# A window-attention and Fourier-mixing kernel: its output turned by VectorE and stored in 16 transfers a band, its planner's count changed

## The chip, the cores and the metric

The kernel runs on one core of a Trainium2 chip. The metric is the device time of one execution in microseconds. All data are float32, apart from a small bias product in bfloat16.

## The reference

The input x is [8, 192, 64, 64]: 8 images, 192 channels, 64 x 64 tokens. Two layers follow one another.

```python
# layer 0
s = layer_norm(tokens)                      # over the 192 channels
q, k, v = qkv(windows of 8 x 8 tokens of s) # 6 heads of 32
a = normalize(q) @ normalize(k).T * temperature
a = where(a >= its 16th largest in the row, a, -100)
x2 = s + proj(softmax(a + rpb) @ v)
x2 = x2 + fc2(gelu(fc1(layer_norm(x2))))    # hidden 768
# layer 1
f = fft2(layer_norm(x2))                    # over 64 x 64, per channel
f = two-layer net on (real, imag) of each value, hidden 16, gelu
y = x2 + ifft2(f).real
out = y + mlp2(gelu(mlp1(layer_norm(y))))   # hidden 768, biases included
```

The output has channels first again, [8, 192, 64, 64].

## The kernel before

Each image is cut into 8 bands of 8 image rows, 512 tokens; so there are 64 bands. A band goes through `front` (load, turn to tokens, layer norm, q, k and v), two `attention` halves, and `back` (projection, the first MLP, statistics for layer 1). When all bands of an image are through, 12 blocks of 16 channels go through `forward`, `pointwise` and `inverse`: the Fourier transform and its inverse as matrix products, with the small net between. Then `leave` takes each band j of image b through the second MLP and out.

Both MLPs are in `mlp` (L743). It takes token-major data (128 tokens on the partitions, 384 numbers of two token groups side by side), normalizes into xa, and turns it to channel-major hn. For layer 1, and for layer 0 from image 1 on, the turn goes over DRAM: VectorE transposes 32 x 32 blocks (lt, L756), SP writes them with four transfers (lr, L765) and fetches them with three (hn, L768 and L770). The first product is mh (L807 and L820), its gelu is on ScalarE (L791), and the second product is mo (L853), token-major again in PSUM.

In `leave` VectorE then adds mo and the residual xy into zt (L1479). TensorE transposes zt with six instructions into the PSUM tile pz (`to_channels`, L731 and L736), ScalarE adds the last bias MLP2B while it moves pz into z (L1491), and SP stores z with three transfers (L1494 and L1496), contiguous over 256 or 512 tokens of a channel.

Tags name pools of buffers: ps, four PSUM tiles that all products share; hn, two channel-major strips (used by hn and by z); att, five tiles (attention scores, their transposes, and lt); h, seven tiles of gelu results; xa, two.

The order is made by a planner in the kernel's own Python code, before anything is recorded. Every step is a `yield op(engine, weight, ...)` with an engine, a duration in units of 10 ns, the buffers it takes and frees, and what it waits for. `Plan.run` (L215) steps through these, engine by engine, choosing by a key that is the possible start plus the task's place, where a place is the image number with fractions for the band or block. `Plan.search` (L278) looks 4000 units ahead 80 times with random noise on the keys, values each draw by TensorE's weight inside that horizon plus 0.15 times that of the others, runs 2000 units with the best, and goes on. The result is an order for every engine, SP's queue included; the queues run in that order, and each instruction waits for its data. Buffers that a step frees come back 15 units after its end, 150 after a DMA.

The constants of layer 1 are loaded in `setup_layer1` (L606), all inside one step that the planner counts as 0 on GpSimd. The gains n1g go there in eight transfers of single numbers (L640). The weights of the second MLP, wmlp, are loaded at its end by `load_mlp` (L458), also uncounted.

Of the kernel before, what the change touches and what calls it, by code (L numbers as in the profile page):

```python
# [9 lines left out]
FP = mybir.dt.float32  # L10
# [3 lines left out]
ALU = mybir.AluOpType  # L14
# [115 lines left out]
class Plan:  # L130
# [84 lines left out]
    def run(self, until, noise=None):  # L215
        ops, clock, mode, units = self.ops, self.clock, self.mode, self.units
        at, front, place, ready = self.at, self.front, self.place, self.ready
        while ready:
# [48 lines left out]
            for name in put:  # L267
                units[name].append(end + (150 if engine == "sp" else 15))
                units[name].sort()
# [7 lines left out]

    def search(self, tries=80, step=2000, horizon=4000, spread=25):  # L278
        draw = random.Random(1)
        now = 0  # L280
        while self.ready:
            now = max(now, self.clock["pe"])
            kept, best = self.save(), None
            for k in range(tries):
                seed = draw.random()
                noise = drawn(seed, spread) if k else None
                if not self.run(now + horizon, noise):
                    self.restore(kept)
                    continue
                worth = 0  # L290
                for _, _, engine, begin, weight in self.log[kept[-1]:]:
                    part = min(weight, max(0, now + horizon - begin))
                    worth += part if engine == "pe" else 0.15 * part
                if not self.ready:
                    worth = 1e9 - max(self.clock.values())
                if best is None or worth > best[0]:
                    best = worth, seed if k else None
                self.restore(kept)
            seed = best[1]
            self.run(now + step, drawn(seed, spread) if seed is not None else None)  # L300
            now += step
        return [(self.names[task], engine, number) for number, task, engine, _, _ in self.log]


# [37 lines left out]
def program(ctx, tc, x, out, w):  # L342
# [108 lines left out]
    for h in range(6):  # L451
        src = bass.AP(w["rpb"].tensor, w["rpb"].offset + h * 225, [[15, 8], [1, 8], [1, 113]])
        nc.sync.dma_start(rrev[64 * (h // 3) : 64 * (h // 3) + 64, h % 3, 0:113], src)
    wides = spare("wides", [128, 3, 2, 128])
    qb_parts = spare("qb_parts", [1, 3, 2 * C], BF)
# [12 lines left out]
    for t in range(2):  # L468
# [5 lines left out]
    wproj = [ctile(f"wprojr_{k}", [128, 64 + C]) for k in range(2)]  # L474
    alongs = {name: ctile(name, [128, 2 * C]) for name in ("gain1", "bias1", "bias2")}
    gain1, bias1, bias2 = (
        t.unsqueeze(1).to_broadcast([128, 2, 2 * C]) for t in alongs.values()
# [40 lines left out]
    def setup_rows():  # L518

        yield op("pe", 20, "full", get="ps", after=["vbias", (None, 1700)])
        pv = psum("pvp")
        times(pv[:, 0, 0:1], wproj_raw, slice(0, CA), vbias)
        times(pv[0:64, 1, 0:1], wproj_raw, slice(CA, C), vbias)
        yield op("dve", 90, put="ps")
        for k, n in enumerate((CA, 64)):
            for v in (pv[0:n, k, 0:1], vec(B1)[k][0:n]):
                nc.vector.tensor_tensor(pbias[k][0:n], pbias[k][0:n], v, ALU.add)


        yield op("dve", 110, put="h h")
        for k, t in enumerate(wproj):
            nc.vector.tensor_copy(t[:, 64:], wproj_raw[k])
            nc.vector.tensor_copy(t[:, 0:64], wproj_raw[k][:, CA:C])
        vectors = (vec(G1), pbias, vec(FC2B))
        yield op("dve", 150)
        for wide, v in zip((wides[:, i] for i in range(3)), vectors):
            for k, n in enumerate((CA, 64)):
                nc.vector.tensor_copy(wide[0:n, k, :], v[k][0:n].to_broadcast([n, 128]))  # L540
        yield op("pe", 60, "full", get="ps", put="h")
        pt = psum("along")
        for i in range(3):
            for k, n in enumerate((CA, 64)):
                to = pt[:, i // 2, i % 2 * C + k * CA : i % 2 * C + k * CA + n]
                nc.tensor.transpose(to, wides[0:n, i, k, :], ident[0:n, 0:n])
        yield op("dve", 270, put="ps", done="rows")
        for i, t in enumerate(alongs.values()):
            of = pt[:, i // 2, i % 2 * C : (i % 2 + 1) * C]
            nc.vector.tensor_copy(t[:, 0:C], of)  # L550
            nc.vector.tensor_copy(t[:, C : C + 64], of[:, CA:C])
            nc.vector.tensor_copy(t[:, C + 64 :], of[:, 0:CA])
# [53 lines left out]
    def setup_layer1():  # L606
        yield op("pool", 0, get="xf", after=[("att", 0, 0, 1)])
        for j, name in enumerate(("fcos", "fsin")):
# [3 lines left out]
            for e in range(2):  # L612
                own = w[name][64 * e : 64 * e + 64]
                for c in range(2):
                    rows = 64 * c + 32 * e
                    nc.sync.dma_start(ihalf[j][rows : rows + 32], own[0:32])

        for t in range(4):
            row = 64 * (t % 2) + 32
            nc.sync.dma_start(ihalf[1][32 * t : 32 * t + 1], w["fcos"][row : row + 1])  # L620
        for k in range(4):
            src = w["fwd2"].rearrange("(a b k e) v -> k b a e v", a=2, k=4, e=2)[k]
            nc.sync.dma_start(frow[8 * k : 8 * k + 8], src)
        for c in range(1, 4):
            nc.sync.dma_start(frow[32 * c : 32 * c + 32], frow[0:32])
        inv1 = sb.tile([128, 128], FP, tag="xf", name="inv1", bufs=1)
        nc.sync.dma_start(inv1, w["inv1"])
# [4 lines left out]
        nc.sync.dma_start(ab, w["ab"])  # L632
        n1t = w["n1"]
        for c in range(2):
            for k in range(4):
                src = bass.AP(
                    n1t.tensor, n1t.offset + c * 2 * HC + k, [[0, 32], [4, 24], [1, 1]]
                )
                dst = n1g[32 * k : 32 * k + 32, 24 * c : 24 * c + 24]
                nc.sync.dma_start(dst.unsqueeze(2), src)  # L640
            nc.sync.dma_start(n1b2[:, c, :], w["n1"][c : c + 1, 1, :])
        yield op("dve", 120, after=[("att", 0, 1, 1)])
        for e in range(2):
# [29 lines left out]
        nc.vector.tensor_scalar(dc, ab[0:1, 1:2], float(HW), None, ALU.mult)  # L673
        nc.vector.tensor_scalar(n1b2, n1b2, float(HW), None, ALU.mult)
        wmlp.extend(load_mlp("wmlp1", "wmlp2"))

# [63 lines left out]
    def flat(name):  # L740
        return psum(name).rearrange("p k n -> p (k n)")

    def mlp(src, nm, w1, fc1_bias, w2, by_dma, then=None):  # L743

# [6 lines left out]
        if by_dma:  # L751
            ready = yield op("dve", 101, get="att rows", put="xa", after=last)
            turned = sb.tile([128, 6, 2, 2, 32], FP, tag="att", name=f"lt_{nm}", bufs=ATT_BUFS)
            whole = to.rearrange("p j (g k) -> p j g k", k=32)
            for t, g, c, n in ((0, 0, 0, 6), (1, 6, 4, 2), (1, 8, 0, 4)):
                nc.vector.transpose(  # L756
                    turned[:, c : c + n, t].rearrange("p g j k -> p j g k"),
                    whole[:, :, g : g + n],
                )
            yield op("sp", 200, put="att")  # L760
# [100 lines left out]
        return acc, last  # L861


    def loading(b, i):
# [5 lines left out]
    def front(b, i):  # L870
# [97 lines left out]

        def by_block(half, p):

            return half.rearrange("c (n b) -> c b n", b=2)[:, p]

        def qk_a(pq, p, first):
            for t in range(2):
                tok = by_block(xn[:, t * HALF : (t + 1) * HALF], p)
                nc.tensor.matmul(  # L976
                    pq[:, t, : 2 * C],
                    tok,
                    wqkv[0][:, : 2 * C],
                    start=first,  # L980
                    stop=not first,
                    skip_group_check=True,
                )

        def qk_b(pq, p, first):
            flags = dict(skip_group_check=True, stop=not first)
            for t in range(2):
                rows = slice(64 * t, 64 * t + 64)
                tok = by_block(xn[rows, BAND:ROW], p)
# [100 lines left out]
    def attention(b, i, hb):  # L1090
# [41 lines left out]
        for k0 in range(0, 12, 2):  # L1132
            yield op("dve", 90, get="sm" if k0 == 0 else "")
            if k0 == 0:
                top = small([128, 3, 4, 16], "top")
            rows = [(s[:, k // 4, k % 4], top[:, k // 4, k % 4]) for k in (k0, k0 + 1)]
            rest = [
                sb.tile([128, 64], FP, tag="s2", name=f"s2_{nm}_{k0 + k}", bufs=4) for k in range(2)
            ]
# [322 lines left out]
    def leave(b, j):  # L1462
# [3 lines left out]
        if j == 0:  # L1466
# [4 lines left out]
        yield op("pool", 0, after=blocks + [("dc", b), ("mlp", 1)])  # L1471
        xy = xys[b][0]
        acc, last = yield from mlp(
            lambda t, q: xy[:, t, q, j, :], f"d{nm}", wmlp[0], fcb[:, 1, :], wmlp[1], True
        )
        left[b] -= 1
        yield op("dve", 88, get="xa", put="ps xy" if left[b] == 0 else "ps")
        zt, pair = tokens("xa", 2, f"zt_{nm}")
# [4 lines left out]
            ALU.add,  # L1483
        )
        yield op("pe", 66, "full", get="ps hn", put="xa")
        pz = flat(f"pz_{nm}")
# [27 lines left out]
        ([(setup_layer1(), 0.2)], 1),  # L1514
        ([(setup_mlp(1, lambda: wmlp, *layer1, ["layer1", ("att", 0, 5, 1)]), 0.2)], 1),
        ([(front(b, i), at_band(b, i, -.12)) for b, i in bands], 1),
# [88 lines left out]
```

## Time and profile before

| | us |
|---|---|
| median of 3 runs | 4598.14 |
| lowest and highest | 4592.67, 4598.62 |
| profiled execution | 4606.84 |
| its span | 4605.0 |
| TensorE busy | 4377.8 |
| VectorE busy | 2769.9 |
| ScalarE busy | 2506.5 |
| GpSimd busy | 2337.6 |
| mean granted TensorE clock | 0.984 |

The profile is one execution; its span runs from the first to the last instruction. PE is TensorE, PEld its weight loads, DVE VectorE, ACT ScalarE, POOL GpSimd, and SPq the queue from which SP issues DMAs. A line of a group names the source line, engine, operation, written and read tile and shape; then busy time, mean duration in ns, and the idle time just before it with what ended it. A float32 product counts two instructions in the profile, a transpose one. In a table by stretches each engine has its busy time and its number of instructions; behind them stand the granted clock, the mean busy share of the 16 DMA engines and GB/s. In a timeline a line has the start, the length, the engine, and how many instructions were merged. For a tile's or a line's instructions the durations are lowest, median and highest in ns.

### The profile page before, as it was taken

Reading aid. Unit: us, or ns where it says so; the run is one execution under the profiler, and the core shown is the slowest. Engines: PE = TensorE matmul, PEld = TensorE weight load, DVE = VectorE, ACT = ScalarE, POOL = GpSimd, SP = SyncE. Lnnn points to the kernel's source line nnn. Section 1 sums busy time; section 2 is a strip of 40 time slices with the busy share of each in tenths; the row PEclk is TensorE's granted clock in tenths of the full one; section 3 lists DMA queues with packets and bytes.
Section 4 is the critical chain, followed back from the end, with each engine's and each line's share of the span. In section 5 each row is a group of like instructions: output and inputs, shape, how many; then the busy total and the mean of one; then the engine's idle time right before and its main releaser. Section 6 shows DMA issues by size and latency. Waiting matters only on the chain. (4 is left out here: it accounts for less than half of the span.)

```text
span 4605.0 us, 143865 instructions
## 1 busy us (share of the span) xinstructions
PE 4377.8 (95%) x60506; PEld 3470.0 (75%) x60506; DVE 2769.9 (60%) x11070; ACT 2506.5 (54%) x3693; POOL 2337.6 (51%) x2161
## 2 busy tenths in 40 slices
PE   7888999999999999999999999999999999999989
PEld 5777777887778777778767877778777787778758
DVE  7888776746774466763767456774576744742111
ACT  4555666545663456544656446564566544653552
POOL 7787765525564365652756246663375533631100
PEclk8999999999999999999999999999999999999999
DMA  2001221311123111221122211222112221111002
GB/s 55 16 12 50 57 60 41 98 52 43 50 57 94 49 47 47 67 73 50 47 56 63 71 50 54 57 64 71 56 47 57 74 63 43 47 47 52 19 19 66
DMA packets 271072, 246.42 MB, mean 54 GB/s; under 512 B 39983, under 2 KB 223482, under 8 KB 270426
## 3 DMA queue, kind: packets, MB, share of 16 engines
q1 hardware_dynamic: 270414, 237.22, 18.6%
q8 instruction: 476, 7.80, 0.7%
q14 instruction: 170, 1.39, 0.1%
q10 hardware_dynamic: 12, 0.00, 0.0%
HBM read 120.52 MB, written 116.39 MB: 51 GB/s over the span
## 5 line engine op out<-in xcount | busy, mean ns | idle before, releaser
L1349 ACT ACTIVATE fh<-fh,ab 128x1024 f32<-128x1024 f32 x768 | 814.1, 1113 | 374.3 <-PE fh L1366 372.0
L960 POOL TENSOR_TENSOR nrm<-nrm,mhalf 128x24 f32<-128x24 f32 x128 | 549.0, 4289 | 10.7
L853 PE MATMUL mo_b<-wfc,h_b 128*128 128x192 f32 x3072 | 529.1, 330 | 1.2 <-ACT fh L1349 1.0
L853 PE MATMUL mo_d<-wmlp,h_d 128*128 128x192 f32 x3072 | 514.2, 327 | 2.7 <-ACT h_d L791 2.6
L853 PEld LDWEIGHTS mo_b<-wfc,h_b 128*128 128x128 f32 x3072 | 502.4, 191 | 14.3 <-issue 6.9
L853 PEld LDWEIGHTS mo_d<-wmlp,h_d 128*128 128x128 f32 x3072 | 498.6, 190 | 11.3 <-ACT h_d L791 4.8
L1153 POOL TENSOR_TENSOR s<-s,top 128x768 f32<-128x768 f32 x128 | 193.7, 1514 | 602.9 <-DVE s L1150 452.3
L1366 PE MATMUL fh<-fz,w1p 32*128 32x264 f32 (+1 forms) x6144 | 454.5, 401 | 10.8 <-issue 2.9
L791 ACT ACTIVATE h_d<-mh_d,fcb 128x512 f32<-128x512 f32 x384 | 241.0, 686 | 286.3 <-PE mh_d L820 221.7
L1366 PEld LDWEIGHTS fh<-fz,w1p 32*128 32x128 f32 x6144 | 288.0, 184 | 144.0 <-issue 79.6
L1393 PE MATMUL fo<-fh,w2p 128*32 128x248 f32 (+1 forms) x6144 | 384.3, 385 | 9.3 <-issue 3.8
L807 PE MATMUL mh_b<-hn_b,wfc_a 128*128 128x256 f32 x1536 | 375.6, 390 | 15.7 <-DMA hn_b<-lr_b 5.7
L807 PE MATMUL mh_d<-hn_d,wmlp_a 128*128 128x256 f32 x1536 | 363.0, 386 | 18.8 <-DMA hn_d<-lr_d 16.8
L807 PEld LDWEIGHTS mh_d<-hn_d,wmlp_a 128*128 128x128 f32 x1536 | 284.5, 190 | 79.9 <-issue 39.4
L807 PEld LDWEIGHTS mh_b<-hn_b,wfc_a 128*128 128x128 f32 x1536 | 279.5, 190 | 85.2 <-issue 30.1
L1143 DVE MATCH_REPLACE8 s<-top,s 128x64 f32<-128x64 f32 x1536 | 309.8, 209 | 0.0
L1393 PEld LDWEIGHTS fo<-fh,w2p 128*32 128x32 f32 x6144 | 188.6, 110 | 154.1 <-issue 29.4
L1479 DVE TENSOR_TENSOR zt<-mo_d,xy 128x768 f32<-128x768 f32 x64 | 61.0, 952 | 396.9 <-PE mo_d L853 396.5
L1163 POOL TENSOR_TENSOR s<-s,rsum 128x768 f32<-128x768 f32 x128 | 192.6, 1508 | 207.3 <-DVE rsum L1161 159.2
L791 ACT ACTIVATE h_b<-mh_b,fcb 128x512 f32<-128x512 f32 x384 | 239.5, 692 | 86.5 <-PE mh_b L820 72.3
L1141 DVE MAX8 top<-s 128x8 f32<-128x64 f32 x1536 | 256.9, 209 | 42.1 <-ACT s L1041 41.3
L702 POOL TENSOR_SCALAR rs_d<-mv_d 128x4 f32<-128x4 f32 x64 | 14.6, 229 | 526.2 <-DVE mv_d L695 504.0
(213 smaller groups left out, 8716.9 us busy)
## 6 DMA issues: line engine op xcount, KB each, us to landing
ar<-tt SPq DMA_DIRECT2D x448, 96.0 KB
at<-ar SPq DMA_DIRECT2D x112, 384.0 KB
lr_d<-lt_d SPq DMA_DIRECT2D x256, 96.0 KB
lr_b<-lt_b SPq DMA_DIRECT2D x224, 96.0 KB
xin<-in_x SPq DMA_DIRECT2D x64, 256.0 KB
hn_d<-lr_d SPq DMA_DIRECT2D x64, 256.0 KB
out<-z SPq DMA_DIRECT2D x64, 256.0 KB
hn_b<-lr_b SPq DMA_DIRECT2D x56, 256.0 KB
```

What stands on the lines that cost most here:

```text
L791: nc.scalar.activation(to, of, AF.Gelu, bias=fc1_bias[:, 2 * fp + k : 2 * fp + k + 1],)
L807: nc.tensor.matmul(ph[:, t, k * HALF : (k + 1) * HALF], w1[0][:, f], hn[:, t * HALF : (t + 1) * HALF], start=(first and k == 0), stop=not ...
L853: nc.tensor.matmul(acc[:, j, t * C : (t + 1) * C], hs[f // 2][:, f % 2, q * 128 : (q + 1) * 128], w2[:, f, ORDER[t]], start=(f == 0 and t ...
L960: nc.gpsimd.tensor_tensor(nf, nf, mhalf[:, :24], ALU.pow)
L1141: nc.vector.max(best[:, 0:8], of)
L1143: nc.vector.match_replace(s2, best[:, 0:8], of, -3.0e38)
L1153: nc.gpsimd.tensor_tensor(s, s, top[:, :, :, 0:1].to_broadcast(shape), ALU.subtract)
L1163: nc.gpsimd.tensor_tensor(s, s, row(rsum), ALU.mult)
L1349: nc.scalar.activation(hs[hf, k], ph, AF.Gelu, bias=ab[:, 0:1])
L1366: nc.tensor.matmul(phs[k // 2][:, k % 2, cols], w1p[i][rows, hf].rearrange("p h v -> p (h v)"), fz[rows, :] if rhs is None else zu[rows, : ...
L1393: nc.tensor.matmul(po[rows, :] if i == 0 else pou[rows, :, 1 : U - 1], w2p[i][:, hf].rearrange("p a v -> p (a v)"), hs[hf, k // 2][:, k % ...
L1479: nc.vector.tensor_tensor(zt.rearrange("p j (t c) -> p j t c", t=2), acc[:, :, : 2 * C].rearrange("p j (t c) -> p j t c", t=2), xy[:, :, : ...
```

## The change

In `leave` all bands but the last two of the last image take a new way out. GpSimd adds the last bias to xy while the MLP runs (bias3, a fourth row built at setup beside gain1, bias1 and bias2). VectorE adds mo and xy into zt, and transposes zt's 32 x 32 blocks into a tile of the att pool, with three instructions. SP stores that tile with 16 transfers, each of 32 partitions with 6 pieces of 32 numbers, in two planned steps of eight. The transposes on TensorE and the two activations on ScalarE remain for two bands only.

The planner draws 100 times, weighs each step's work by an exponential of how far its place lies behind the place that TensorE's work has reached, counts the other engines' work at 0.05, gives buffers back with the engine's own arrival time, and can step back where no draw goes through. The loads of `setup_layer1` are steps on SP with durations; n1g is made from two broadcast loads and four copies on VectorE. Attention's scratch rows s2 have two buffers instead of four.

```diff
@@ run
-                units[name].append(end + (150 if engine == "sp" else 15))
+                units[name].append(end + (150 if engine == "sp" else ARRIVES[engine]))
@@ search
-    def search(self, tries=80, step=2000, horizon=4000, spread=25):
+    def search(self, tries=100, step=2000, horizon=4000, spread=25, mu=2.0, wt=0.05):
...
+            done += sum(v[4] for v in self.log[counted:] if v[2] == "pe")
+            counted = len(self.log)
+            here = course[bisect.bisect(course, (done,))][1] if done < course[-1][0] else course[-1][1]
+            value = [math.exp(mu * (here - place) / 360) for place in self.place]
...
-                    part = min(weight, max(0, now + horizon - begin))
-                    worth += part if engine == "pe" else 0.15 * part
+                        part = min(weight, max(0, now + horizon - begin)) * value[task]
+                        worth += part if engine == "pe" else wt * part
...
@@ setup_layer1
-        yield op("pool", 0, get="xf", after=[("att", 0, 0, 1)])
+        yield op("sp", 420, get="xf", after=[("att", 0, 0, 1)])
...
-            for k in range(4):
-                src = bass.AP(
-                    n1t.tensor, n1t.offset + c * 2 * HC + k, [[0, 32], [4, 24], [1, 1]]
-                )
-                dst = n1g[32 * k : 32 * k + 32, 24 * c : 24 * c + 24]
-                nc.sync.dma_start(dst.unsqueeze(2), src)
+            of = w["n1"][c, 0, :].partition_broadcast(128)
+            nc.sync.dma_start(gains[:, c * HC : (c + 1) * HC], of)
...
+        yield op("dve", 60, after=[last])
+        for k in range(4):
+            rows = slice(32 * k, 32 * k + 32)
+            of = gains[rows].rearrange("p (n k) -> p k n", k=4)[:, k]
+            nc.vector.tensor_copy(n1g[rows], of)
...
+        yield op("sp", 200, done="wmlp")
         wmlp.extend(load_mlp("wmlp1", "wmlp2"))
...
+    def quarters(tensor, b, i, half):
+        band = tensor[b, :, 8 * i : 8 * i + 8, :].rearrange("(g k) r s -> k g (r s)", k=32)
+        for a in (2 * half, 2 * half + 1):
+            for q in range(4):
+                yield band[:, :, 128 * q + 32 * a : 128 * q + 32 * a + 32], q, a
...
@@ attention
-                sb.tile([128, 64], FP, tag="s2", name=f"s2_{nm}_{k0 + k}", bufs=4) for k in range(2)
+                sb.tile([128, 64], FP, tag="s2", name=f"s2_{nm}_{k0 + k}", bufs=2) for k in range(2)
@@ leave
+        turned_out = (b, j) < (B - 1, NB - 2)
+
+        def biased():
+            yield op("pool", 178, done=("biased d", b, j))
+            for t in range(2):
+                rows = xy[:, t, :, j, :]
+                nc.gpsimd.tensor_tensor(rows, rows, bias3[:, :, t * C : (t + 1) * C], ALU.add)
...
+            biased if turned_out else None,
...
+            after=[last, ("biased d", b, j)] if turned_out else None,
...
+        if turned_out:
+            yield op("dve", 101, get="att", put="xa")
+            turned = sb.tile([128, 6, 2, 2, 32], FP, tag="att", name=f"z_{nm}", bufs=ATT_BUFS)
+            for of, into in zip(by_chunk(zt), by_block(turned)):
+                nc.vector.transpose(into, of)
+            of = turned.rearrange("p g t j k -> p (t j) g k")
+            for half in range(2):
+                yield op("sp", 368, put="att" if half else "")
+                for into, q, a in quarters(out, b, j, half):
+                    nc.sync.dma_start(into, of[32 * a : 32 * a + 32, q])
+            return
         yield op("pe", 66, "full", get="ps hn", put="xa")
...
@@ streams
-        ([(setup_mlp(1, lambda: wmlp, *layer1, ["layer1", ("att", 0, 5, 1)]), 0.2)], 1),
+        ([(setup_mlp(1, lambda: wmlp, *layer1, ["wmlp"]), 0.2)], 1),
```

More of the change, by code (lines that the diff above doesn't have):

```diff
@@ L1 @@
+import bisect
+import math
 import random
@@ L276, in run @@
         return True
-    def search(self, tries=80, step=2000, horizon=4000, spread=25):
+    def search(self, tries=100, step=2000, horizon=4000, spread=25, mu=2.0, wt=0.05):
         draw = random.Random(1)
-        now = 0
+        now = done = counted = 0
+        course = self.course()
+        history = []
         while self.ready:
             now = max(now, self.clock["pe"])
+            done += sum(v[4] for v in self.log[counted:] if v[2] == "pe")
+            counted = len(self.log)
+            here = course[bisect.bisect(course, (done,))][1] if done < course[-1][0] else course[-1][1]
+            value = [math.exp(mu * (here - place) / 360) for place in self.place]
@@ L283, in search @@
             kept, best = self.save(), None
             for k in range(tries):
[L285 to L291, printed above, removed]
-                    part = min(weight, max(0, now + horizon - begin))
-                    worth += part if engine == "pe" else 0.15 * part
@@ L294, in search @@
[L294 to L297, printed above, removed]
-                self.restore(kept)
-            seed = best[1]
-            self.run(now + step, drawn(seed, spread) if seed is not None else None)
+                seed = draw.random() if k else None
+                if self.run(now + horizon, seed and drawn(seed, spread)):
+                    worth = 0
+                    for _, task, engine, begin, weight in self.log[kept[-1]:]:
+                        part = min(weight, max(0, now + horizon - begin)) * value[task]
+                        worth += part if engine == "pe" else wt * part
+                    if not self.ready:
+                        worth = 1e9 - max(self.clock.values())
+                    if best is None or worth > best[0]:
+                        best = worth, seed
@@ L301, in search, with course @@
+                self.restore(kept)
+            if best is None:
+                kept, now, done, counted = history[-min(3, len(history))]
+                del history[-3:]
+                self.restore(kept)
+                continue
+            history.append((kept, now, done, counted))
+            self.run(now + step, best[1] and drawn(best[1], spread))
             now += step
         return [(self.names[task], engine, number) for number, task, engine, _, _ in self.log]
+    def course(self):
+        work = []
+        for place, numbers in zip(self.place, self.lists):
+            engines = [self.ops[number][0][0] for number in numbers]
+            work.append((place, sum(weight for engine, weight in engines if engine == "pe")))
+        course, total = [], 0
+        for place, weight in sorted(work):
+            total += weight
+            course.append((total, place))
+        return course
@@ L453, in program @@
         nc.sync.dma_start(rrev[64 * (h // 3) : 64 * (h // 3) + 64, h % 3, 0:113], src)
-    wides = spare("wides", [128, 3, 2, 128])
+    wides = spare("wides", [128, 4, 2, 128])
     qb_parts = spare("qb_parts", [1, 3, 2 * C], BF)
@@ L474, in program @@
     wproj = [ctile(f"wprojr_{k}", [128, 64 + C]) for k in range(2)]
-    alongs = {name: ctile(name, [128, 2 * C]) for name in ("gain1", "bias1", "bias2")}
-    gain1, bias1, bias2 = (
+    alongs = {name: ctile(name, [128, 2 * C]) for name in ("gain1", "bias1", "bias2", "bias3")}
+    gain1, bias1, bias2, bias3 = (
         t.unsqueeze(1).to_broadcast([128, 2, 2 * C]) for t in alongs.values()
@@ L535, in setup_rows @@
             nc.vector.tensor_copy(t[:, 0:64], wproj_raw[k][:, CA:C])
-        vectors = (vec(G1), pbias, vec(FC2B))
+        vectors = (vec(G1), pbias, vec(FC2B), vec(MLP2B))
         yield op("dve", 150)
-        for wide, v in zip((wides[:, i] for i in range(3)), vectors):
+        for wide, v in zip((wides[:, i] for i in range(4)), vectors):
             for k, n in enumerate((CA, 64)):
@@ L542, in setup_rows @@
         pt = psum("along")
-        for i in range(3):
+        for i in range(4):
             for k, n in enumerate((CA, 64)):
@@ L616, in setup_layer1 @@
                     nc.sync.dma_start(ihalf[j][rows : rows + 32], own[0:32])
+        yield op("sp", 280)
         for t in range(4):
@@ L623, in setup_layer1 @@
             nc.sync.dma_start(frow[8 * k : 8 * k + 8], src)
+        yield op("sp", 180)
         for c in range(1, 4):
             nc.sync.dma_start(frow[32 * c : 32 * c + 32], frow[0:32])
-        inv1 = sb.tile([128, 128], FP, tag="xf", name="inv1", bufs=1)
+        yield op("sp", 280)
+        first = sb.tile([128, 128 + C], FP, tag="xf", name="first", bufs=1)
+        inv1, gains = first[:, 0:128], first[:, 128:]
         nc.sync.dma_start(inv1, w["inv1"])
@@ L632, in setup_layer1 @@
         nc.sync.dma_start(ab, w["ab"])
-        n1t = w["n1"]
+        last = yield op("sp", 180)
         for c in range(2):
-            for k in range(4):
-                src = bass.AP(
-                    n1t.tensor, n1t.offset + c * 2 * HC + k, [[0, 32], [4, 24], [1, 1]]
-                )
-                dst = n1g[32 * k : 32 * k + 32, 24 * c : 24 * c + 24]
-                nc.sync.dma_start(dst.unsqueeze(2), src)
-            nc.sync.dma_start(n1b2[:, c, :], w["n1"][c : c + 1, 1, :])
-        yield op("dve", 120, after=[("att", 0, 1, 1)])
+            of = w["n1"][c, 0, :].partition_broadcast(128)
+            nc.sync.dma_start(gains[:, c * HC : (c + 1) * HC], of)
+            nc.sync.dma_start(n1b2[:, c, :], w["n1"][c : c + 1, 1, :])
+        yield op("dve", 60, after=[last])
[3 more added lines that the diff above has]
+            nc.vector.tensor_copy(n1g[rows], of)
+        yield op("dve", 120)
         for e in range(2):
@@ L741, in flat, with by_chunk, by_block @@
         return psum(name).rearrange("p k n -> p (k n)")
+    PARTS = (0, 0, 0, 6), (1, 6, 4, 2), (1, 8, 0, 4)
+    def by_chunk(tile_):
+        blocks = tile_.rearrange("p j (g k) -> p j g k", k=32)
+        return [blocks[:, :, g : g + n] for _, g, _, n in PARTS]
+    def by_block(turned):
+        return [turned[:, c : c + n, t].rearrange("p g j k -> p j g k") for t, _, c, n in PARTS]
     def mlp(src, nm, w1, fc1_bias, w2, by_dma, then=None):
@@ L753, in mlp @@
             turned = sb.tile([128, 6, 2, 2, 32], FP, tag="att", name=f"lt_{nm}", bufs=ATT_BUFS)
[L754 to L759, printed above, removed]
+            for of, into in zip(by_chunk(to), by_block(turned)):
+                nc.vector.transpose(into, of)
             yield op("sp", 200, put="att")
@@ L967, in values, with by_row @@
             copy(done, vv.rearrange("p t a c -> p t (a c)"), pv[:, :, : 2 * C])
-        def by_block(half, p):
+        def by_row(half, p):
             return half.rearrange("c (n b) -> c b n", b=2)[:, p]
@@ L974, in qk_a @@
             for t in range(2):
-                tok = by_block(xn[:, t * HALF : (t + 1) * HALF], p)
+                tok = by_row(xn[:, t * HALF : (t + 1) * HALF], p)
                 nc.tensor.matmul(
@@ L988, in qk_b @@
                 rows = slice(64 * t, 64 * t + 64)
-                tok = by_block(xn[rows, BAND:ROW], p)
+                tok = by_row(xn[rows, BAND:ROW], p)
                 nc.tensor.matmul(
@@ L1472, in leave @@
         xy = xys[b][0]
-        acc, last = yield from mlp(
-            lambda t, q: xy[:, t, q, j, :], f"d{nm}", wmlp[0], fcb[:, 1, :], wmlp[1], True
+        turned_out = (b, j) < (B - 1, NB - 2)
[4 more added lines that the diff above has]
+                nc.gpsimd.tensor_tensor(rows, rows, bias3[:, :, t * C : (t + 1) * C], ALU.add)
+        acc, last = yield from mlp(
+            lambda t, q: xy[:, t, q, j, :],
+            f"d{nm}",
+            wmlp[0],
+            fcb[:, 1, :],
+            wmlp[1],
+            True,
+            biased if turned_out else None,
         )
         left[b] -= 1
-        yield op("dve", 88, get="xa", put="ps xy" if left[b] == 0 else "ps")
+        yield op(
+            "dve",
+            88,
+            get="xa",
+            put="ps xy" if left[b] == 0 else "ps",
+            after=[last, ("biased d", b, j)] if turned_out else None,
+        )
         zt, pair = tokens("xa", 2, f"zt_{nm}")
@@ L1484, in leave @@
         )
+        if turned_out:
+            yield op("dve", 101, get="att", put="xa")
+            turned = sb.tile([128, 6, 2, 2, 32], FP, tag="att", name=f"z_{nm}", bufs=ATT_BUFS)
+            for of, into in zip(by_chunk(zt), by_block(turned)):
+                nc.vector.transpose(into, of)
+            of = turned.rearrange("p g t j k -> p (t j) g k")
[4 more added lines that the diff above has]
+            return
         yield op("pe", 66, "full", get="ps hn", put="xa")
```

## The prediction

> **What bounds the kernel now.** I read the busy table first, then the row of slices, the chain that ended last, and TensorE's busy time in three stretches that I chose: image 0 before its Fourier blocks start, the middle, and the last 461 us.
>
> ```profile
> PE 4377.8 (95%) x60506; PEld 3470.0 (75%) x60506; DVE 2769.9 (60%) x11070; ACT 2506.5 (54%) x3693; POOL 2337.6 (51%) x2161
> PE   7888999999999999999999999999999999999989
> ...
> PE 18%; POOL 1%; ACT 1%; DVE 1%; issue 1%; DMA 0%; SPq 0%; ACTq 0%; POOLq 0%; DVEq 0%
> ...
> 0.00:460.00 460.00, 389.32 (x4718) 309.20 (x4718) 361.55 (x1578) 241.99 (x411) 349.82 (x304) 0.90 0.13 33
> 460.00:4144.00 3684.00, 3557.74 (x50564) 2813.24 (x50561) 2315.12 (x9216) 2065.01 (x3004) 1935.32 (x1779) 0.99 0.21 58
> 4144.00:4605.00 461.00, 430.70 (x5230) 347.56 (x5228) 93.19 (x277) 199.50 (x279) 52.44 (x78) 0.98 0.14 39
> ```
>
> TensorE works in 95% of the span, and the chain that ended last, as far as it was followed back, is nearly all TensorE. Its idle time is 460 - 389.3 = 70.7 us in the first stretch, 3684 - 3557.7 = 126.3 us in the middle and 461 - 430.7 = 30.3 us at the end, 227 us together. In the first stretch VectorE (361.6 of 460) and GpSimd (349.8) are the fuller partners. So a microsecond of TensorE work that leaves is a microsecond of time, unless something new keeps TensorE waiting; work added to the other four engines is free while they stay off its path.
>
> **The part that pays: TensorE's six transposes per band.** Of 64 bands, 62 lose the group pz.
>
> ```profile
> L731 PE MATMUL pz<-ident,zt 128*128 128x128 f32 x256 | 40.5, 281 | 4.7 <-DVE zt L1479 4.5
> L736 PE MATMUL pz<-ident,zt 128*128 128x128 f32 x128 | 24.4, 273 | 0.0
> ...
> 4513.07 1.89 PE L807 MATMUL mh_d<-hn_d,wmlp_a 128*128 128x256 f32 x8
> 4514.80 0.60 PE L731 MATMUL pz<-ident,zt 128*128 128x128 f32 x4
> 4515.23 0.38 PE L736 MATMUL pz<-ident,zt 128*128 128x128 f32 x2
> 4515.54 2.00 PE L820 MATMUL mh_d<-hn_d,wmlp_b 64*128 64x256 f32 x16
> ```
>
> The mean of 281 ns is not the price, since matmuls overlap. The price is how much earlier the next matmul could have begun: the group starts at 4514.80 and the next one at 4515.54, 0.74 us. From below, the weight loads of one group take 0.42 + 0.25 = 0.67 us; from above, a group in the middle of the run (2703.26, next start 2704.25) costs 0.99 us, of which about 0.35 is a wait that the next consumer may take over. I take 0.74, as nothing waits in that stretch: 62 x 0.74 = 45.9 us, ends 41.5 and 61.4. The 4.7 us of idle ahead of pz stay out of the sum. In the built order TensorE has exactly these groups fewer, and two small transposes more at setup (about 0.3 us each by the setup's rows, left out).
>
> **Parts that lie beside TensorE.** ScalarE loses the two activations of z (0.688 + 0.468 us), 62 x 1.156 = 72 us. VectorE gains three block transposes a band; the same shapes for lt_d take 0.573 + 0.269 + 0.402 = 1.244 us, 62 times 77 us, which brings it to 2847 us, 62% of the new time. GpSimd gains two additions of 384 elements a band, by half of its 1.82 us for 768 elements (bias2, L1241) 62 x 1.82 = 113 us, to 2451 us, 54%. The addition of zt now waits for this bias as well; behind it on VectorE would stand the next attention's steps. But the bias is released by the normalized copy, before the block is turned, sent out, fetched and multiplied, more than 15 us ahead of zt, so I put the wait at 0; if GpSimd were 15 us behind, zt would hold its PSUM tile, one of four, that much longer. The removed group also held a PSUM tile and one of the two hn buffers, and the new one holds one of five att buffers through its store. I price that exchange at 0, inside the bounds of the plan below. Two scratch buffers s2 instead of four cost 0: the same engine writes and reads them in order. The wider setup tile and fourth row add a few VectorE copies before image 0's end.
>
> Here a rule of the Trainium skill (SBUF — State Buffer, "Who interferes with whom") speaks against the change: VectorE with two inputs in SBUF and GpSimd reading SBUF exclude each other for a whole instruction. The rows fit it.
>
> ```profile
> L1098 DVE TENSOR_TENSOR qk<-qk,nrm 128x768 f32<-128x768 f32 x97 | 136.3, 1405 | 156.1 <-POOL nrm L961 155.8
> L1479 DVE TENSOR_TENSOR zt<-mo_d,xy 128x768 f32<-128x768 f32 x64 | 61.0, 952 | 396.9 <-PE mo_d L853 396.5
> ```
>
> With one input in PSUM 768 elements take 952 ns; with both in SBUF the mean is 1405. By the row such exclusion has cost 97 x 0.45 = 44 us and TensorE is still 95% busy; by the rule at its worst all 113 us of new additions block VectorE, which makes it (2847 + 113)/4552 = 65% busy. Neither moves the sum. I take 0.
>
> **The store.** SP issued three transfers a band for out; now 16, each of 32 partitions x 6 pieces of 32 numbers: 192 pieces of 128 bytes, 3072 a band. The row with as many pieces is the write of lt_d, 192 of 512 bytes.
>
> ```profile
> L765 SPq DMA_DIRECT2D lr_d<-lt_d x256: 302/455/2055, 806.2 to 4572.0; - x128
> ...
> 73.10 6.10 SPq L640 DMA_DIRECT2D n1g<-in_n x4
> ...
> 80.80 16.05 SPq L640 DMA_DIRECT2D n1g<-in_n x4
> ...
> 4516.36 0.36 SPq L1494 DMA_DIRECT2D out<-z  x1
> 4516.77 1.59 SPq L1496 DMA_DIRECT2D out<-z  x2
> 4519.58 1.82 SPq L765 DMA_DIRECT2D lr_d<-lt_d  x4
> 4522.97 0.34 SPq L768 DMA_DIRECT2D hn_d<-lr_d  x1
> 4523.36 1.11 SPq L770 DMA_DIRECT2D hn_d<-lr_d  x2
> ```
>
> At 0.455 us each, 16 take 7.3 us of SP. The other end is the setup load n1g: four transfers of 768 pieces, also 3072, held SP for 6.1 us on an empty queue and for 16.05 us right behind, so pieces can be the limit. I take 7.3, because the lr_d row has the same count, the same direction and four times the bytes; 16.05 bounds it above.
>
> What stands behind these 16 on SP are the loads at, hn and xin. The last bands show it, where nothing else covers. There mo_d of a band ended at 4513.07, and the load of the band after next was needed at 4530.09. Now: zt ends at 4514.23, the turn takes about 1.2 (4515.5), 16 issues end at 4522.8, the four lr_d at 4524.6, hn may issue 1.57 later (as from 4521.40 to 4522.97), and the data releases TensorE 2.95 after the first hn issue (4493.02 to 4495.97 a period earlier): 4529.1. TensorE, without pz, is there at 4530.09 - 0.74 = 4529.35. So it just fits: 0 at 7.3 us. At 16.05 us each such link is 8.8 us late, and three links follow one another (bands 1, 3, 5 release 3, 5, 7): 26 us. In the middle the plan puts other work over this; I take 0 there too, and give the open size to the rival below.
>
> The rule against it (the Trainium skill, DMA: Bandwidth & Descriptors, "Specifications") says that transfers under 512 bytes are read, modified and written. In the trace, 17 us of the tail hold one lr_d write, one hn load and one out store at a DMA share of 0.24: 0.24 x 16 x 17 = 65 us of engine time; an xin load of hn's size takes 0.15 x 16 x 10 = 24 us (290 to 300 us), which leaves 17 us for 768 pieces, 22.5 ns each of 512 bytes. If the rule makes a 128-byte piece twice that, an estimate, 12 pieces on each of 16 engines take 0.54 us a transfer: 8.6 us a band, and (8.6 - 7.3) x 3 = 4 us in the tail. By the row 0. I take the row; no run here shows a 128-byte write.
>
> **Setup.** Before, SP's unplanned setup ran from 58 to 112 us and delayed xin to 97.4. Still, in 20 to 460 us no wait of TensorE for xin is left on the list, so the gain from moving it behind band 4's load and replacing the eight scattered transfers by two plus four copies is 0; layer 1's constants are not needed before 396 us, where the first block's scaling ran.
>
> **The plan.** New values, 100 draws and other release times reorder everything. In the two built orders TensorE changes its array shape 1797 times before and 1769 after, and image 0 has as little to fill it as before. I see no reason for a sign: 0, with bounds of a third of the middle's idle time gained (-42 us) and a quarter lost (+32).
>
> **Sum.** The profiled execution took 4606.84 us (span 4605.0 and 1.8 around it); 4606.8 - 45.9 = 4560.9. It stands 8.7 above the median of the runs, 4598.14; on the median's footing the forecast is 4552 us.
>
> **Rivals.** *The plan gains too:* a third of the middle's idle, 4598 - 46 - 42 = 4510. For it: the freed PSUM tile, hn buffer and 72 us of ScalarE; against: attention and TensorE's own sum bind as before. *The pieces are the limit (slower):* SP is held 16.05 us a band. Tail +26; in the middle 56 bursts are each 8.8 us longer, and if as many reach TensorE as loads that it waited for before (at 22, hn_d 6, hn_b 4 of 232, 14%), +69: 4598 - 46 + 95 = 4647. It decides where a burst is 7.3 + d with d x (3 + 56 x 0.14) = 46, so d = 4.2: from 11.5 us a band on it is no longer faster. For it n1g's 16.05, against it lr_d. *No change:* a burst near 11.5 us, or a plan that loses all it won: 4598. *The plan loses a quarter of the middle's idle:* 4598 - 46 + 32 = 4584, still faster.
>
> **How the numbers follow.** Chances: the likeliest (4536 to 4568 by the ends of pz and a few us of plan) 0.50; the plan gains 0.24; it loses 0.12; no change 0.06; pieces 0.08. A measurement of this kernel tells about 0.2%, 9 us, from no change. So faster 0.86, same 0.06, slower 0.08. The range runs from 4508, just below the plan's gain, to 4594, above its loss.
>
> **What would show it.** Right: pz only twice, TensorE's busy time near 4378 - 50, idle near 227, z's stores at 0.45 us on SP, waits of mh_d for hn_d in the tail under 2 us. Wrong: stores at 0.7 us and more, long waits of po for at and mh for hn, or the middle's idle far from 126 us.

## The result and the profile after

The changed kernel takes 4531.27 us in the median (4528.59 to 4540.86), the one before 4595.94 in the runs beside it. The ratio is 0.9862, with a 95% interval of 0.9846 to 0.9877: 64.7 us or 1.4% faster, well clear of the 0.2% that a measurement can tell. The forecast was 4552. The sign and the range held; the gain is 1.4 times the one forecast and lies just outside the stretch that was called likeliest, 4536 to 4568. The experiments below show that it has terms which the forecast put at nothing.

The page of the changed kernel (busy time, TensorE's and VectorE's slices, the chain), and TensorE's busy time in the same three stretches as before:

```profile
PE 4306.3 (95%) x60136; PEld 3421.9 (76%) x60136; DVE 2837.5 (63%) x11202; ACT 2457.6 (54%) x3633; POOL 2448.2 (54%) x2274
...
PE   7888999999999999999999999999999999999989
...
DVE  6777677657666667665767576766667756662112
...
PE 16%; DVE 2%; DMA 1%; POOL 1%; SPq 1%; issue 1%; ACT 1%; ACTq 0%; DVEq 0%; POOLq 0%
...
0.00:460.00 460.00, 380.07 (x4720) 298.64 (x4721) 350.21 (x1553) 237.80 (x409) 343.04 (x296) 0.89 0.13 32
460.00:4144.00 3684.00, 3572.38 (x50674) 2845.60 (x50674) 2404.57 (x9405) 2055.69 (x3013) 2042.88 (x1901) 0.99 0.23 59
4144.00:4529.00 385.00, 353.84 (x4748) 277.69 (x4744) 82.68 (x246) 164.10 (x213) 62.32 (x78) 0.98 0.15 34
```

The span fell by 76 us in these two profiled executions (4605.0 to 4529.0; the medians differ by less). TensorE's busy time fell by 71.5 and its idle time only by 4.5, from 227.2 to 222.7. TensorE still sets the time. VectorE and GpSimd ended where the prediction put them (2837.5 against 2847, 2448.2 against 2451).

The group pz, the stores' issues, and the last bands on SP and on TensorE:

```profile
L759 PE MATMUL pz<-ident,zt 128*128 128x128 f32 x8 | 1.3, 279 | 1.1 <-DVE zt L1545 1.1
L764 PE MATMUL pz<-ident,zt 128*128 128x128 f32 x4 | 0.8, 272 | 0.0
...
L1560 SPq DMA_DIRECT2D out<-z x992: 315/440/2042, 804.9 to 4497.8; - x199
...
4406.26 8.55 SPq L1560 DMA_DIRECT2D out<-z  x16
4414.90 1.87 SPq L802 DMA_DIRECT2D lr_d<-lt_d  x4
4418.44 0.34 SPq L805 DMA_DIRECT2D hn_d<-lr_d  x1
...
4411.13 8.07 PE L890 MATMUL mo_d<-wmlp,h_d 128*128 128x192 f32 x48
4421.31 2.63 PE L844 MATMUL mh_d<-hn_d,wmlp_a 128*128 128x256 f32 x8 [2.11 <-DMA hn_d<-lr_d]
```

The transposes are gone but for two bands. The issue of a store costs SP 0.440 us in the median, and a burst of 16 takes 7.6 to 8.7 us in the last bands. The first burst there ends at 4414.81, the write and load behind it follow, and TensorE waits 2.11 us for that load. Behind the later bursts it waits hardly or not at all:

```profile
4439.38 1.89 PE L844 MATMUL mh_d<-hn_d,wmlp_a 128*128 128x256 f32 x8
4455.75 1.89 PE L844 MATMUL mh_d<-hn_d,wmlp_a 128*128 128x256 f32 x8
...
4457.55 8.35 SPq L1560 DMA_DIRECT2D out<-z  x16
...
4472.44 1.97 PE L844 MATMUL mh_d<-hn_d,wmlp_a 128*128 128x256 f32 x8 [0.16 <-DMA hn_d<-lr_d]
```

From the start of a first product to that of the same one a band later, TensorE takes 16.37 us here (4439.38 to 4455.75), against 17.02 before (4513.07 to 4530.09): 0.65 us less without the group pz.

### The profile page after: what moved, and what is told of

Same layout as the page of the kernel before. It is cut to its first block, busy times and chain, and to the rows that moved or that the text cites. A ratio compares the mean times of both kernels' runs of the same rounds, so it can differ in the third digit from the quotient of the medians.

```text
span 4529.0 us, 144394 instructions
## 1 busy us (share of the span) xinstructions
PE 4306.3 (95%) x60136; PEld 3421.9 (76%) x60136; DVE 2837.5 (63%) x11202; ACT 2457.6 (54%) x3633; POOL 2448.2 (54%) x2274
## 5 line engine op out<-in xcount | busy, mean ns | idle before, releaser
L1412 PE MATMUL fh<-fz,w1p 32*128 32x248 f32 (+1 forms) x6144 | 447.0, 401 | 6.6 <-DVE fz L1382 2.5
L1439 PE MATMUL fo<-fh,w2p 128*32 128x264 f32 (+1 forms) x6144 | 383.1, 386 | 7.0 <-issue 4.1
L1187 DVE MAX8 top<-s 128x8 f32<-128x64 f32 x1536 | 256.1, 208 | 44.1 <-ACT s L1087 43.7
L1144 DVE TENSOR_TENSOR qk<-qk,nrm 128x768 f32<-128x768 f32 x106 | 157.4, 1485 | 195.8 <-POOL nrm L1007 195.8
L1191 DVE MAX8 top<-s 128x8 f32<-128x64 f32 x1536 | 265.3, 214 | 0.0
```

Source lines behind the costliest of these rows:

```text
L1187: nc.vector.max(best[:, 0:8], of)
L1191: nc.vector.max(best[:, 8:16], s2)
L1412: nc.tensor.matmul(phs[k // 2][:, k % 2, cols], w1p[i][rows, hf].rearrange("p h v -> p (h v)"), fz[rows, :] if rhs is None else zu[rows, : ...
L1439: nc.tensor.matmul(po[rows, :] if i == 0 else pou[rows, :, 1 : U - 1], w2p[i][:, hf].rearrange("p a v -> p (a v)"), hs[hf, k // 2][:, k % ...
```

## The experiments

All times below are medians of device time; ratios are to the kernel before, run beside them.

**The new way out alone.** Planner and setup are those of before.

```diff
@@ the changed kernel
-    def search(self, tries=100, step=2000, horizon=4000, spread=25, mu=2.0, wt=0.05):
+    def search(self, tries=80, step=2000, horizon=4000, spread=25):
...
-                units[name].append(end + (150 if engine == "sp" else ARRIVES[engine]))
+                units[name].append(end + (150 if engine == "sp" else 15))
...
-        yield op("sp", 420, get="xf", after=[("att", 0, 0, 1)])
+        yield op("pool", 0, get="xf", after=[("att", 0, 0, 1)])
...
```

> The new way out (block transposes, 16 stores, bias on GpSimd) with the planner and the setup of before. Theory A, a group of transposes is worth 0.74 us and the other 19 us of the 65 came from the planner: 4596 - 46 = 4550 us. Theory B, a group is worth 65/62 = 1.04 us and the planner nothing: about 4531 us. TensorE busy: A 4332, B 4310.

Measured: 4557.89 us, ratio 0.9923 (0.9908 to 0.9938), TensorE busy 4334.8. Both sit by theory A (4550 and 4332). But the new steps gave the planner other steps to draw from, so this is another order of the old planner too. Such orders lie up to 62 us apart, as the other starts below show, so this run alone doesn't tell A from B; the doubled transposes do.

**The new planner alone**, with the old way out and setup.

```diff
@@ the kernel before
+    def search(self, tries=100, step=2000, horizon=4000, spread=25, mu=2.0, wt=0.05):
...
+                        part = min(weight, max(0, now + horizon - begin)) * value[task]
+                        worth += part if engine == "pe" else wt * part
...
```

> The new planner with the old way out and the old setup. Theory A: 4596 - 19 = 4577 us. Theory B: 4596 us, within 9. If planner and way out only pay together, 4596 or above here too.

Measured: 4555.83 us, ratio 0.9916 (0.9901 to 0.9931). That is 37 us, twice what theory A had left for it. The instructions of TensorE are those of before, yet its busy time is 39 us less. (The two profiled executions lie 57.5 us apart, more than the medians: 39 of busy and 18 of idle time.) The busy table of this run:

```profile
PE 4338.7 (95%) x60506; PEld 3459.7 (76%) x60506; DVE 2771.5 (61%) x11078; ACT 2497.4 (55%) x3684; POOL 2331.0 (51%) x2158
```

Its weight loads fell by only 10 us (3470.0 to 3459.7), with the same 60506 of them. So most of the 39 us does not look like matmul work. A matmul of 128 x 192 is drawn 327 to 330 ns long where 48 of them follow at 0.165; a wait of one or two tenths of a microsecond behind them can hide under such an end and is counted as busy. An estimate of what hides: take each group of matmuls from its start to the next group's start, less the idle time that the profile marks, and compare it with the lower quartile of the same group in the kernel before. Between 460 and 4100 us this excess is 99.5 us before and 60.8 with the new planner. Up to 10 us of that difference is clock (the time missing to a full granted clock is 20.5 us there against 10.2). The idle marked as such fell from 123.2 to 95.7 us. That the excess is hidden waiting is inferred; the trace doesn't mark it.

**The setup alone.**

```diff
@@ the kernel before
-        yield op("pool", 0, get="xf", after=[("att", 0, 0, 1)])
+        yield op("sp", 420, get="xf", after=[("att", 0, 0, 1)])
...
+            of = w["n1"][c, 0, :].partition_broadcast(128)
...
```

> The planned setup transfers alone, with the old planner and the old way out. Both theories: 4596 us within 9, since TensorE never waited for a load that the old setup delayed; a gain of over 9 us would say that the setup's place in the prediction was wrong.

Measured: 4628.42 us, ratio 1.0076 (1.0058 to 1.0093), 35 us slower. The edit's own instructions can't explain it: in the first 460 us TensorE's idle is 72.0 us, against 70.7. What grew is the middle and the last stretch, hundreds of microseconds after the setup. The planned durations change the draws that come after, so this run posed the question whether one order says anything of an edit.

**The transposes twice**, with the order held.

```diff
         to_channels(pz, pair, zt)
+        to_channels(pz, pair, zt)
```

> The kernel before with the six transposes of every band issued twice and the plan, so the order, held: 64 groups more. At 0.74 us each (theory A) +47, 4643 us; at 1.04 (theory B) +66, 4662 us; at the weight loads' 0.67 us +43.

Measured: 4636.26 us, ratio 1.0090 (1.0075 to 1.0105): 43.2 us for 64 groups, 0.675 us each, by the interval 0.54 to 0.75. This is the cleanest price of the group, as the order is held: 62 of them are worth 42 us, by the interval 33 to 47. Theory B is out.

**Other draws of the same planners.**

```diff
-        draw = random.Random(1)
+        draw = random.Random(2)
```

> The kernel before with the planner's random numbers started from 2 instead of 1; nothing else changes. If the 37 us of the new planner alone are its rule's, this stays within 12 us of 4593. If they are the luck of one order, orders of one planner scatter by 20 us and more, so 4573 or less, or 4613 or more, is to be seen here or with start 3.

> The same with start 3: within 12 us of 4593 by the rule, 20 us and more away by luck. The setup alone, which gave 4628, changed the order too, and speaks for luck.

> The changed kernel with the random numbers started from 2. If the rule is what pays: within 12 us of 4531. If start 1 was a lucky order: 4545 to 4560, which is before less the 42 us of the transposes with some scatter.

> The same with start 3: 4519 to 4543 if the rule pays, 4545 to 4560 if start 1 was lucky.

| start of the random numbers | kernel before, us | changed kernel, us |
|---|---|---|
| 1 | 4593 to 4597 | 4531.27 |
| 2 | 4655.55 | 4526.92 |
| 3 | 4617.52 | 4534.10 |

Each of the two explanations, luck and rule, holds for one planner. The old one scatters by luck, over 62 us, and the order of the kernel before is the best of its three. The new planner's three orders lie within 7 us, inside each other's intervals. So the setup alone (4628) is one more order of the old planner, and no verdict on the setup.

**The planner without the weight by place.** The other edits to the planner stay.

```diff
@@ the new planner alone
-    def search(self, tries=100, step=2000, horizon=4000, spread=25, mu=2.0, wt=0.05):
+    def search(self, tries=100, step=2000, horizon=4000, spread=25, mu=0.0, wt=0.05):
```

> The new planner alone (as in the run with it alone, 4556 us) with the weight by place switched off: every step counts its full duration again; 100 draws, 0.05 for the other engines and the release times stay. If counting by place is what makes the orders good and alike, this falls back among the old planner's orders: 4593 to 4655. If the other three edits do it, 4556 within 12.

Measured: 4656.64 us, ratio 1.0132 (1.0117 to 1.0148). It falls back among the old orders, to their slow end. The weight by place is what pays; 100 draws, the 0.05 and the release times give nothing that shows in this one order, and one order of a planner that scatters by 62 us can't show a small gain. The excess of the estimate above is about 107 us in this run and 109 in start 2, but 69 in the changed kernel, where the clock took about as much as before (18.8 us). What the weight does can be read from VectorE's slices. The first page is that of the kernel before, the second that of its start 2, the third the planner without the weight by place, the fourth the new planner alone:

```profile
DVE  7888776746774466763767456774576744742111
```

```profile
DVE  6878777627775476744776347773576734832111
```

```profile
DVE  7777767745765567665767448573676636742111
```

```profile
DVE  7877777656766666656666647764577547652111
```

VectorE's work comes mostly from attention. Where only the sum inside the horizon counts, bands of the second MLP are taken in bunches with little attention beside them, and VectorE swings, between 3 and 7 tenths in the middle of the kernel before and between 2 and 8 in its start 2, about once per image. With the weight by place it stays nearer to 6. In 39 equal stretches from 460 to 4051.9 us the standard deviation of VectorE's share is 0.128 in the kernel before, 0.157 and 0.153 in its starts 2 and 3, 0.130 without the weight by place, and 0.087, 0.075, 0.079 and 0.103 in the new planner alone and the changed kernel's three starts. So the orders with the weight are both evener and faster than all those without it. Among those without it evenness doesn't rank the times: 0.128 goes with 4593 us and 0.130 with 4657. That the even mix is the cause, rather than a sign of it, is argued and not shown.

**Three long stores in place of 16**, order held.

```diff
-                for into, q, a in quarters(out, b, j, half):
-                    nc.sync.dma_start(into, of[32 * a : 32 * a + 32, q])
+                whole = turned.rearrange("p g t j k -> p (g t j k)")
+                rows = out[b, :, 8 * j : 8 * j + 8, :]
+                if half == 0:
+                    nc.sync.dma_start(rows[0:CA], whole[:, :BAND].rearrange("p (r s) -> p r s", s=HW))
+                    continue
+                for t in range(2):
...
```

> The changed kernel with the same order on every engine, but each turned tile is stored by three long transfers (256 and 2 x 64 KB) in place of 16; the numbers land in other places of the band, so the output is not the reference's. It prices the 16 transfers. The prediction's term, 0: 4531 us within 9. If the 3072 short pieces reach TensorE through late loads, this is faster by the two us of wait in the tail and by part of the 41 us that TensorE waits for at: 4500 to 4520.

Measured: 4514.05 us, ratio 0.9823 (0.9808 to 0.9838), which doesn't overlap the changed kernel's interval: the 16 short transfers cost about 17 us (8 to 28 by the two intervals). Only 2 us of it is the tail's long wait, which is gone here. The wait for at is hardly shorter (39.8 against 40.9 us), so that half of the expectation failed. By what ended them, TensorE's waits fall by 5 us for DMAs, 9 for VectorE and 1 for GpSimd, and those for ScalarE rise by 3; in the middle 7 us less is missing to a full clock (11.9 against 18.8). It is a little everywhere, and which transfer starts it is open.

**Pieces half as long, twice as many**, order held.

```diff
-                    nc.sync.dma_start(into, of[32 * a : 32 * a + 32, q])
...
+                        into = band[4 * q + a].rearrange("i (k n) -> k i n", n=16)
+                        nc.sync.dma_start(into, whole[32 * a : 32 * a + 32, :, 16 * q : 16 * q + 16])
```

> The changed kernel with the order held and 16 transfers a band, each of 384 pieces of 64 bytes instead of 192 of 128; the numbers land in other places of the band, so the output is not the reference's. If the issue on SP sets the burst's length (0.44 us each, 7 us), nothing moves: 4531 within 9. If pieces set it, the burst goes from 7 to about 15 us: some 20 us from three links in the tail and some tens in the middle, 4560 to 4620.

Measured: 4537.98 us, ratio 0.9872 (0.9856 to 0.9886); the interval overlaps the changed kernel's. The stores' issues in this run and two of its bursts:

```profile
L1564 SPq DMA_DIRECT2D out<-z x992: 315/468/2033, 806.7 to 4503.9; - x199
...
4445.67 8.01 SPq L1564 DMA_DIRECT2D out<-z  x16
...
4462.04 9.18 SPq L1564 DMA_DIRECT2D out<-z  x16
```

With 384 pieces a transfer takes SP 0.468 us instead of 0.440, and a burst in the last bands 8.0 to 9.2 us instead of 7.6 to 8.7. Twice the pieces hardly move it, so issuing sets the burst.

**Without the last bias**, order held.

```diff
-                nc.gpsimd.tensor_tensor(rows, rows, bias3[:, :, t * C : (t + 1) * C], ALU.add)
+                pass
```

> The changed kernel with the order held and GpSimd's two additions of the last bias left out of every band (the bias is left out of the sum). The prediction priced them at 0: 4531 us within 9. If they held VectorE or GpSimd's later steps up on TensorE's path: up to 20 us faster, 4511.

Measured: 4525.97 us, ratio 0.9849 (0.9833 to 0.9865). GpSimd's busy time fell from 2448.2 to 2329.1, so each band's two additions take 1.92 us. The time is 5 us shorter, and the interval overlaps the changed kernel's. VectorE's product qk, with both inputs in SBUF, takes 1489 ns in the mean here and 1485 in the changed kernel, so the additions don't hold it up.

## Why the prediction was right, point by point

The sign and the mechanism of the part that pays were right. That the number came so near was in part luck: two terms put at nothing, a gain of 37 us and a cost of 17, left 20 us between them, and the start of the kernel before was the best of three. Between equal starts 2 and 3 the change is worth 129 and 83 us.

*What bounds.* Right: TensorE's work is 95% of the time, before and after.

*The transposes, 0.74 us a group.* Right in mechanism; 0.675 by doubling them, and 0.65 by the step of the last bands, so 62 are worth about 42 us, not 45.9. Both lie by the weight loads' 0.67, which the prediction had as its lower end; the interval, 0.54 to 0.75, just holds 0.74 too.

*"The plan ... I see no reason for a sign: 0".* This step failed. From the same start the new planner gives 37 us (32 to 45 by the interval), close to the bound of 42. The rival "the plan gains too" had the direction right, but for a freed tile and buffer, which are not needed for it: the gain is there with the old way out. The step compared changes of array shape, 1797 against 1769, which hardly differ, and took its bounds from idle time alone; of the 57.5 us between the two profiled executions 39 lay in time that the profile counts as busy. Nor did it ask how far two orders of one planner lie apart: 62 us in three, more than the gain that was forecast and nearly as much as the one measured. The slices of VectorE, 7446676376 in the middle, were on the page and not used.

*The store, 0.* Right that SP's issues, and not the pieces, set the burst: 0.440 us against 0.455. But the term is about 17 us, not 0. In the tail "it just fits" held for the order that it was worked out in: behind a burst of 8.35 us TensorE waited 0.16. The one wait there of more, 2.11 us, comes mainly from another order. In the prediction's link TensorE had work for 16.3 us after mo_d; here it had work for 14.7 (from 4404.48 until its wait began at 4419.20). The data came 16.8 us after mo_d and not 16.0, although the burst took 8.55 and not 7.3. In the middle, where most of the 17 us lie, plan and other work did not cover everything. The bursts ended below the prediction's deciding 11.5 us, so the slower rival did not come.

*The rule on transfers under 512 bytes* (the Trainium skill, DMA: Bandwidth & Descriptors, "Specifications"). The prediction took a 512-byte piece at 22.5 ns and, as its estimate of the rule, a 128-byte one at twice that, 45 ns. The packets in the traces give both. The changed kernel's 190592 packets of 128 bytes took a DMA engine 12.1 ns each in the mean, and its 92548 of 512 bytes, nearly all of them the writes lr_b and lr_d, 30.9 ns. With half pieces the 381184 packets of 64 bytes took 9.6 ns. So the 22.5 was too low, and the doubling wrong: a piece of 128 bytes costs 1.6 times as much per byte as one of 512, but only 0.4 times as much per piece. Twelve of them on an engine, 0.15 us, hide behind an issue of 0.44. Had the doubling been right, the measured 30.9 ns would have made 0.74 us a transfer and 11.9 us a band, past the 11.5. The row of lr_d was the better guide; why a read-modify-write doesn't show is not known from these runs.

*VectorE, GpSimd, ScalarE beside it.* VectorE and GpSimd as forecast. ScalarE fell by 49, not 72: steps that either ScalarE or VectorE can take moved to it. The shared-port rule: GpSimd's additions cost at most 5 us, not told from 0, and qk is no longer with them.

*Setup, 0.* Open. Alone it was measured in one order of a planner that scatters by 60 us, and in the first 460 us it changed TensorE's idle by 1.3.

*The sum.* -42 for the transposes, -37 for the planner from this start, +17 for the stores: -62 of the measured -65. From the planner alone it closes as well: 4556 - 42 + 17 = 4531. Each term is known to 7 to 10 us, and they were measured in different orders, so that it closes this well is chance in part. Against the mean of the old planner's three orders, 4622, the change is worth 91 us.

## What to carry to other kernels

When an edit goes through a search, hold the order and change only the work, or try several starts, before a gain or a loss is put down to the edit. Where an engine is 95% busy, look at what its groups advance by, not at its idle time alone, for short waits can be drawn as work. And if a planner counts work inside a window, see that it doesn't eat one kind of work first: an uneven row of another engine's slices is a first sign, though not a measure of the loss.

## What the runs showed of the hardware that was not expected

Two programs with the same 60506 matmuls differ by 39 us in TensorE's busy time (4377.8 and 4338.7) and by 10 in its weight loads in the profile; up to 14 us of it may be the granted clock, to whose full rate 75 us are missing over the one span and 61 over the other. A group of six 128 x 128 float32 transposes inside a full stream costs 0.675 us, 0.11 each, though one is drawn 0.27 long. A DMA piece of 64 or 128 bytes written from SBUF to DRAM took 9.6 and 12.1 ns of a DMA engine, where one of 512 took 30.9. The issue of a transfer from SP hardly depends on its pieces at these sizes: 0.440 us in the median with 192 of 128 bytes, 0.468 with 384 of 64, 0.455 with 192 of 512.
